# Layer 0's start: table rows in contiguous pieces, the second image's load on SyncE, tables between the first bands' pieces

## The chip, the cores and the metric

The kernel runs on one core of one Trainium2 chip. The metric is the device time of one execution in microseconds (us), given as the median of several runs. A core has five engines, each with its own instruction stream: TensorE (PE, matrix products and transposes), VectorE (DVE), ScalarE (ACT), GpSimd (POOL) and SyncE (SP, which here only issues DMAs). ScalarE can issue DMAs too; an instruction that issues one and has to wait holds up whatever stands behind it on its engine.

## What is computed

Two images x of 128 channels and 64 x 64 pixels go through two layers. Layer 0 is group norm, then a neighbourhood attention block (4 heads of 32 channels, each pixel looks at a 7 x 7 window, with a learned table of position biases rpb), then two small dense blocks. Layer 1 is a full attention over the 4096 tokens of each image and a spectral convolution in four branches.

```python
x = x + _L0_conv_ref(_gn(x), ...)              # layer 0
t = _to_tokens(x)
t = t + _L1_attn_ref(_ln_t(t))                 # layer 1
t = t + _L1_ffn_ref(_ln_t(t), ...)

# inside layer 0
y = _ln(x, g1, be1)
qkv = (y @ qkv_w.T + qkv_b)                    # q scaled by DH ** -0.5
attn = einsum('bnhwd,bnhwijd->bnhwij', q, Kw)  # Kw, Vw: 7 x 7 windows, moved inside at the border
attn = attn + rpb[:, bih, biw]                 # bih, biw: offset of key from query, 0 to 12
out = einsum('bnhwij,bnhwijd->bnhwd', softmax(attn), Vw)
y = out @ proj_w.T + proj_b
y = _ln(y, g2, be2) @ w1.T + bl1 + r           # r: layer 0's input, then two more dense products
```

The change touches only how the bias table is brought into place, when the second image is loaded, and in what order the first pieces of layer 0's work are issued.

## The kernel before, in words

Layer 0 works in bands of eight image rows, 512 pixels: eight bands for each of the two images, sixteen in all, numbered k = 0 to 15. A band is eight tiles of 8 x 8 pixels; two tiles make a unit, so a band has units u0 to u3. The keys of a tile are a window of 14 x 14 pixels (196). A band's work is cut into named pieces (functions under `@piece`). Those of the first part, called `p.`, are: xg (group norm applied), tok (transpose to tokens), bn, pw, nb, zd, za (layer norm on DVE, POOL, DVE, DVE and ACT), tr and zT (transpose back), then k, q, v (products) and kT, qT, vc (copies out of PSUM). Each unit then has S (scores), t0 to t3 (one per head: scores plus table, with the minimum, on DVE), e0 to e3 (exponential, on ACT), T0, T1 (transposes of p), c0, c1 (their copies) and V (product with v). `r.` and `t.` pieces finish a band; `k.` pieces begin layer 1 for the first image.

The order on PE, DVE, ACT and POOL is written out: every piece gets a time, all are sorted by it, and the engines follow that order. `PLAN` gives a piece's time in its band, and each band is shifted by PERIOD = 2300. The first pieces stand outside of it: the string `FIRST` lists them, and a name's place in it less 1000 is its time. In `FIRST`, `gn` is group norm of image 0, `w` and `wd` the small products that fold biases into weights, `f0` to `f3` bring the table of one head into place, `tab0` to `tab3` make the first table from it on DVE, and `tab` makes twelve more on POOL. Four further steps (`behind`, L747 on, driven by `rest_`) fold the remaining weights; they stand at the times 150, 500, 850 and 1200, that is among the pieces of unit 0 to unit 1 of band 0. `second` (at 1000) loads the second image into `xa[1]` in four pieces, issued by ScalarE (L795). SyncE's order is not written out: it takes its DMAs as they are issued and allowed.

The table. For each head, the host lays rpb into a padded array of RPR = 21 rows of RPW = 128 numbers. A query at row r, column q of its tile needs the 20 x 20 numbers that begin at its own offset in this array. They are loaded so that the query's place is the partition: `rev` has 64 partitions (eight rows r of eight q), and one partition holds, for each head, 20 rows of 20 numbers. For each r two DMAs do it: L290 (heads 1 to 3, on SyncE, or on ScalarE where r is 2 or 5) and L292 (head 0, on ScalarE), with runs of 20 numbers, 80 bytes. `rev` lies in the buffer `cm[0]`, which layer 1 uses later; what lies outside of the padded array is filled by the two memsets at L281 and L282. A product with the constant `flip` (L248) then reverses the order of the queries and doubles it to 128 partitions in PSUM, and ScalarE copies it to `base` (L252). `table` (L254 to L261) subtracts it from the window mask.

The keys and values. `p.vc` copies v and stores it in eight DMAs per band to DRAM (vd, L475), and `windows` (L485 on) loads for each unit four pieces of 7 rows x 14 columns x 128 channels back (vw, L492), sixteen for a band. There are six buffers of vw, four are used by a band. All of these DMAs are issued by SyncE. The rows of a window reach into the neighbouring bands, so a band's loads wait for the next band's stores.

Of the kernel before, what the change touches and what calls it, by code (L numbers as in the profile page):

```python
# [14 lines left out]
P = 128  # L15
# [5 lines left out]
HEADS, DH, KW = 4, 32, 7  # L21
# [9 lines left out]
W_QKV, W_PROJ, W_1, W_2, W_3 = 0, 384, 512, 640, 768  # L31
V_G1, V_BE1, V_G2, V_BE2, V_G3, V_BE3, V_G4, V_BE4, V_QB, V_KB, V_BL3 = range(11)
R_VB, R_PROJ, R_BL1, R_BL2 = range(4)
RPW = 128


QT, WN, NTAB = 8, 14, 20
# [2 lines left out]
BAND = QT * GW  # L40


RPR = NTAB + 1

# [23 lines left out]


FIRST = (
    "gn p.xg0 p.xg1 p.tok0 p.tok1 w p.bn0 p.bn1 p.pw0 p.pw1 p.zd0 p.nb0 p.za0 p.tr0 p.zd1 p.nb1 p.za1 wd p.xg2 p.zT0 f0"
    " p.tr1 f1 p.v0 p.q0 p.k0 p.zT1 p.vc0 p.qT0 tab0 p.kT0 f2 f3 tab p.v1 p.k1 p.q1 tab1 p.vc1 p.kT1 p.qT1 tab2 tab3"
).split()
PHW = P + TH

# [15 lines left out]
def kernel(  # L93
# [16 lines left out]
    nc = tc.nc  # L110
# [12 lines left out]
    xa = [xp.tile([P, T], F32, tag=f"xa{b}", name=f"xa{b}") for b in range(NB)]  # L123
    xin = x.rearrange("b c h w -> b c (h w)")
    for c in range(4):
# [3 lines left out]
    tt, tok, cm = [None, None], [None, None], [None, None]  # L129
# [4 lines left out]
    space = tok[0].rearrange("p n c -> p (n c)")  # L134
    base = space[:, 0 : HEADS * NTAB * NTAB].rearrange("p (h n m) -> p h n m", h=HEADS, n=NTAB)
    mask = space[:, HEADS * NTAB * NTAB : HEADS * NTAB * NTAB + 6 * KEYS].rearrange("p (c k) -> p c k", k=KEYS)
    rev = cm[0][0 : QT * QT, 0 : HEADS * RPR * NTAB].rearrange("p (h n m) -> p h n m", h=HEADS, n=RPR)

    ident = const.tile([P, P], F32, name="ident")
    make_identity(nc, ident)  # L140
# [4 lines left out]
        out=flip, in_=flip, compare_op=ALU.not_equal, fill=1.0, base=1 - QT * QT, pattern=[[0, 2], [1, QT * QT]],  # L145
# [73 lines left out]
    with l0a:  # L219
# [21 lines left out]
        tab = big.tile([P, 6, HEADS, KEYS], F32, name="tab")  # L241
        def l0_bank(kind=0):
            pool, tag = rings[kind]
            return pool.tile([P, 512], F32, tag=tag, name="bank")

        def flipped(h):
            pb = l0_bank()
            nc.tensor.matmul(  # L248
                pb[:, 0 : NTAB * NTAB], lhsT=flip.rearrange("p a q -> p (a q)"),
                rhs=rev[:, h, 0:NTAB].rearrange("p n m -> p (n m)"), start=True, stop=True,  # L250
            )
            nc.scalar.copy(base[:, h].rearrange("p n m -> p (n m)"), pb[:, 0 : NTAB * NTAB])  # L252

        def table(ci, h, eng):  # L254
# [16 lines left out]
            out=gavg, in_=gavg, compare_op=ALU.is_ge, fill=0.0, base=0,  # L271
# [3 lines left out]
            out=gavg, in_=gavg, compare_op=ALU.is_ge, fill=0.0, base=3,  # L275
# [2 lines left out]
        gavg = gavg.rearrange("p g r -> p (g r)")  # L278


        nc.gpsimd.memset(rev[:, 0].rearrange("p n m -> p (n m)"), 0.0)  # L281
        nc.gpsimd.memset(rev[:, HEADS - 1, NTAB], 0.0)  # L282
        nc.sync.dma_start(out=mask, in_=nc.inline_tensor(_window_masks(), "window_masks").ap())
        for r in range(QT):
            lo = 6 - min(r, 6)
            src = bass.AP(
                rpb_pad.tensor, (RPR + r - 6) * RPW + 50, [[1, QT], [RPW, (HEADS - 1) * RPR - r // 7], [1, NTAB]]
            )
            rows_ = rev[r * QT : (r + 1) * QT].rearrange("p h n m -> p (h n) m")
            (nc.scalar if r % 3 == 2 else nc.sync).dma_start(out=rows_[:, RPR : HEADS * RPR - r // 7], in_=src)  # L290
            src = bass.AP(rpb_pad.tensor, (lo + r - 6) * RPW + 50, [[1, QT], [RPW, RPR - lo], [1, NTAB]])
            nc.scalar.dma_start(out=rows_[:, lo:RPR], in_=src)  # L292
        wg = w_sb
        cb = wp.tile([P, 5], F32, name="cb")
        C_Q, C_K, C_V, C_1, C_3 = range(5)
# [476 lines left out]
        events = []  # L772
# [8 lines left out]
        for name, f in (  # L781
            ("gn", lambda: [None for _ in group_norm(0)]), ("w", weights), ("wd", weights_kept),
            *((f"f{h}", lambda h=h: flipped(h)) for h in range(HEADS)),
            *((f"tab{h}", lambda h=h: table(0, h, nc.vector)) for h in range(HEADS)),
            ("tab", lambda: [table(ci, h, nc.gpsimd) for ci in (1, 4, 5) for h in range(HEADS)]),
        ):
            events.append((FIRST.index(name) - 1000, None, "", f))
        for i in range(8):
            events.append((2 * PERIOD + 600 * i, None, "", lambda ci=2 + i // 4, h=i % 4: table(ci, h, nc.gpsimd)))
        rest_ = behind()  # L790
        for i in range(4):
            events.append((150 + 350 * i, None, "", lambda: next(rest_)))
        def second():
            for c in range(4):
                nc.scalar.dma_start(out=xa[1][:, c * 1024 : (c + 1) * 1024], in_=xin[1, :, c * 1024 : (c + 1) * 1024])  # L795

        events.append((1000, None, "", second))

        gn1 = group_norm(1)
        for i in range(7):  # L800
# [569 lines left out]
def _window_masks():  # L1370

    import numpy as np

    def seen(offset):

        q, k = np.arange(QT)[:, None], np.arange(WN)[None, :]
        lo = np.clip(offset + q - 3, 0, WN - KW)
        return (k >= lo) & (k < lo + KW)

    m = np.zeros((2, QT, QT, 6, WN, WN), np.float32)  # L1380
    for ci in range(6):
        rows_ = seen((0, 6, 3)[ci // 2])
        for ab in range(2):
            cols = seen(((0, 6), (3, 3))[ci % 2][ab])
            m[ab, :, :, ci] = np.where(rows_[:, None, :, None] & cols[None, :, None, :], 0.0, -MASKED)
    return m.reshape(P, 6, KEYS)
# [77 lines left out]
```

## Time and profile before

| what | value |
|---|---|
| median of 4 runs | 2264.2 us (2263.33 to 2265.31) |
| profiled execution | 2265.31 us |
| its span in the profile | 2263.6 us |
| granted PE clock, mean | 0.989 |
| DMA queue of SyncE | 177866 packets, 105.47 MB |
| DMA queue of ScalarE | 2840 packets, 2.27 MB |
| DMA issues L475 and L492 | 128 of 32.0 KB, 256 of 49.0 KB |

The profile gives, for each engine, how long it was busy, and for each idle stretch what ended it. A group of instructions is told by its line in the source, the engine, the operation and out<-in. Engine names with a q (SPq, ACTq) are the engines' issuing of DMAs. In a view of stretches, one row is a stretch of time, with the busy time of each engine in it, the clock that PE was granted as a share of full speed, and what the DMA engines moved. The chain of work goes back from the last instruction: at each step to what released it, or to the instruction before it on its engine. Layer 0 fills roughly the first 340 us of the span; the last band's window loads end at 328.

### The profile page before, as it was taken

Reading aid. Unit: us, or ns where it says so; the run is one execution under the profiler, and the core shown is the slowest. Engines: PE = TensorE matmul, PEld = TensorE weight load, DVE = VectorE, ACT = ScalarE, POOL = GpSimd, SP = SyncE. Lnnn points to the kernel's source line nnn. Section 1 sums busy time; section 2 is a strip of 40 time slices with the busy share of each in tenths; the row PEclk is TensorE's granted clock in tenths of the full one; section 3 lists DMA queues with packets and bytes.
Section 4 is the critical chain, followed back from the end, with each engine's and each line's share of the span. In section 5 each row is a group of like instructions: output and inputs, shape, how many; then the busy total and the mean of one; then the engine's idle time right before and its main releaser. Section 6 shows DMA issues by size and latency. Waiting matters only on the chain.

```text
span 2263.6 us, 31741 instructions
## 1 busy us (share of the span) xinstructions
PE 2186.1 (97%) x11908; PEld 1352.1 (60%) x11908; DVE 939.7 (42%) x3047; ACT 785.3 (35%) x1911; POOL 276.9 (12%) x354
## 2 busy tenths in 40 slices
PE   5899998999999999999999979999999999999998
PEld 3677764544544444544444436776677777767777
DVE  4799985432444346433333333222213222232323
ACT  2789883222333223222222323223223222232322
POOL 3367874200000000000000000000000000000000
PEclk8999999999999999999999989999999999999999
DMA  4222213011100015100000133122222121222101
GB/s 116 65 61 61 61 51 50 0 56 56 33 24 24 11 45 153 32 24 23 1 24 24 42 85 91 42 55 58 44 53 58 39 58 39 57 45 52 41 8 75
DMA packets 180858, 109.76 MB, mean 48 GB/s; under 512 B 32225, under 2 KB 165857, under 8 KB 180194
## 3 DMA queue, kind: packets, MB, share of 16 engines
q1 hardware_dynamic: 177866, 105.47, 18.0%
q10 hardware_dynamic: 2840, 2.27, 0.4%
q8 instruction: 94, 1.54, 0.3%
q14 instruction: 58, 0.48, 0.1%
HBM read 73.09 MB, written 34.60 MB: 48 GB/s over the span
## 4 chain that ended last, share of the span: by engine, by line
PE 87%; DVE 5%; POOL 3%; DMA 1%; ACT 1%; issue 1%; SPq 1%; POOLq 0%; DVEq 0%; ACTq 0%
PE acc L1288 25%; PE pc L1277 13%; PE bank L896 10%; PE own L924 10%; PE other L949 8%; PE bank L910 4%; PE bank L331 2%; PE py L1315 2%; PE bank L1041 2%; PE bank L188 2%; PE bank L1009 2%; PE bank L541 1%; PE bank L1150 1%; PE po L563 1%; PE bank L505 1%
## 5 line engine op out<-in xcount | busy, mean ns | idle before, releaser
L1278 DVE COPY y<-pc 128x512 f32<-128x512 f32 x320 | 221.4, 692 | 359.0 <-PE pc L1277 355.3
L903 ACT ACTIVATE e<-bank 128x512 f32<-128x512 f32 x288 | 171.8, 597 | 562.7 <-PE bank L896 426.8
L896 PE MATMUL bank<-cm 128*128 128x512 f32 x576 | 298.0, 601 | 1.4 <-DVE y L652 1.4
L1277 PE MATMUL pc<-ct,ut 64*128 64x512 f32 x1280 | 287.6, 599 | 5.9 <-issue 5.9
L1288 PE MATMUL acc<-y,mpl 128*128 128x256 f32 x1280 | 292.1, 382 | 0.0
L1288 PE MATMUL acc<-y,mmi 128*128 128x256 f32 x1280 | 288.0, 379 | 0.0
L1288 PEld LDWEIGHTS acc<-y,mpl 128*128 128x128 f32 x1280 | 238.1, 190 | 59.4 <-issue 29.6
L1288 PEld LDWEIGHTS acc<-y,mmi 128*128 128x128 f32 x1280 | 242.6, 190 | 32.7
L1278 ACT COPY y<-pc 128x512 f32<-128x512 f32 x320 | 205.2, 641 | 93.7 <-PE pc L1277 93.7
L949 PE MATMUL other<-e,tok 128*128 128x512 f32 x448 | 228.6, 592 | 0.0
L924 PE MATMUL own<-et,tok 128*128 128x512 f32 x448 | 226.9, 593 | 0.7 <-DVE part L913 0.7
L913 DVE CUSTOM_DVE_ANT_0 et<-bank,one 128x512 f32<-128x512 f32 x224 | 145.6, 688 | 164.9 <-PE bank L910 164.8
L1277 PEld LDWEIGHTS pc<-ct,ut 64*128 64x128 f32 x1280 | 122.0, 188 | 152.6 <-issue 147.4
L1294 ACT COPY ob<-acc 128x256 f32<-128x256 f32 x40 | 24.1, 603 | 430.9 <-PE acc L1288 430.9
L924 PEld LDWEIGHTS own<-et,tok 128*128 128x128 f32 x448 | 84.6, 190 | 108.3 <-issue 73.1
L949 PEld LDWEIGHTS other<-e,tok 128*128 128x128 f32 x448 | 85.0, 190 | 106.6 <-issue 105.9
L1327 DVE TENSOR_TENSOR xa<-py,xa 128x512 f32<-128x512 f32 x32 | 22.1, 692 | 281.4 <-PE py L1315 281.4
L896 PEld LDWEIGHTS bank<-cm 128*128 128x128 f32 x576 | 96.0, 193 | 71.2 <-issue 42.7
L910 PEld LDWEIGHTS bank<-ident,e 128*128 128x128 f32 x896 | 103.3, 141 | 54.0 <-issue 45.9
L160 POOL TENSOR_TENSOR ln_rs<-ln_rs,mhalf 128x4 f32<-128x4 f32 x24 | 24.3, 1011 | 869.4 <-DVE ln_rs L159 869.4
L528 ACT ACTIVATE p<-p,mn 128x196 f32<-128x196 f32 x256 | 114.4, 449 | 22.1 <-DVE mn L518 13.7
L910 PE MATMUL bank<-ident,e 128*128 128x128 f32 x896 | 116.9, 273 | 0.0
(200 smaller groups left out, 2338.1 us busy)
## 6 DMA issues: line engine op xcount, KB each, us to landing
ut<-us SPq DMA_DIRECT2D x80, 256.0 KB
us<-ub SPq DMA_DIRECT2D x64, 256.0 KB
vw<-vd SPq DMA_DIRECT2D x256, 49.0 KB
ct<-gs SPq DMA_DIRECT2D x160, 72.0 KB
ct<-gs SPq DMA_DIRECT2D x160, 64.0 KB
gs<-ub SPq DMA_DIRECT2D x20, 256.0 KB
vd<-v SPq DMA_DIRECT2D x128, 32.0 KB
st<-in_m_plus_dram SPq DMA_DIRECT2D x16, 256.0 KB
```

What stands on the lines that cost most here:

```text
L188: nc.tensor.transpose(ps[:, j * P : (j + 1) * P], src[:, j, :], ident)
L331: nc.tensor.matmul(pl, lhsT=wg[:, lo : lo + P], rhs=zT, start=True, stop=True)
L528: nc.scalar.activation(p, p, AF.Exp, bias=t[name + "mn"][:, h : h + 1], scale=-1.0, accum_out=t["den"][:, u, h : h + 1],)
L896: nc.tensor.matmul(ps, lhsT=cm[b][:, n * P : (n + 1) * P], rhs=cm[b][:, chunk(c)], start=True, stop=True)
L903: nc.scalar.activation(e, ps, AF.Exp, bias=0.0, scale=ASCALE, accum_out=part[:, n, c : c + 1])
L910: nc.tensor.transpose(pt[:, k * P : (k + 1) * P], es[k][:, m * P : (m + 1) * P], ident)
L913: nc.vector.tensor_tensor_reduce(et, pt, one, 1.0, 0.0, ALU.mult, ALU.add, part[:, n, a : a + 1])
L924: nc.tensor.matmul(own, lhsT=tok[b][:, n, :], rhs=e, start=first, stop=last)
L949: nc.tensor.matmul(other, lhsT=tok[b][:, 4 * CHUNKS[a] + j, :], rhs=es[j], start=(j == 0), stop=(j == 3))
L1277: nc.tensor.matmul(pc, lhsT=ut[fp, b, par, :], rhs=cv_[fp], start=True, stop=True)
L1278: (nc.scalar.copy if f else nc.vector.tensor_copy)(y[:, 4 * f : 4 * f + 4, :, par, b * 2 * FB + q : (b + 1) * 2 * FB : 2], pc.rearrange("p ...
L1288: nc.tensor.matmul(acc, lhsT=(mmi if l else mpl)[:, k, :], rhs=y[:, 1::2, k, ::-1, :] if l else y[:, 0::2, k, :, :], start=(l == 0 and k = ...
```

## The change

- RPW goes from 128 to 70 and RPR from 21 to 22, so that the padded rows lie closely and what a query needs of a head is one contiguous run of RLEN = 19 x 70 + 20 = 1350 numbers, 5400 bytes. `rev` becomes a list of four places: heads 1 and 2 in `cm[0]`, heads 0 and 3 in `tt[0]`, behind the 3 x 128 numbers that `behind` uses.
- For each r there is one DMA on SyncE (heads 1 and 2, two runs for each of eight partitions) and two on ScalarE (heads 0 and 3, one run for each of eight partitions; head 0's leaves out the rows before the array). One memset stays.
- The product of `f0` to `f3` reads its 20 x 20 numbers out of the run with a row step of 70.
- The second image's four loads go from ScalarE at the time 1000 to SyncE, right behind the row pieces and ahead of the first store of v; `second` is gone.
- In `FIRST`, f0 stands behind w, f1 behind p.za0, f2 behind p.zT0, f3 behind p.tr1, with tab after it; tab0, tab1 and tab2 stand ahead of p.kT0, tab3 ahead of p.v1.
- The four steps of `behind` go from 150, 500, 850, 1200 to 900, 1200, 1500, 1800.

```diff
-RPW = 128
+RPW = 70
-RPR = NTAB + 1
+RPR = NTAB + 2
+RLEN = (NTAB - 1) * RPW + NTAB
 FIRST = (
-    "gn p.xg0 p.xg1 p.tok0 p.tok1 w p.bn0 p.bn1 p.pw0 p.pw1 p.zd0 p.nb0 p.za0 p.tr0 p.zd1 p.nb1 p.za1 wd p.xg2 p.zT0 f0"
-    " p.tr1 f1 p.v0 p.q0 p.k0 p.zT1 p.vc0 p.qT0 tab0 p.kT0 f2 f3 tab p.v1 p.k1 p.q1 tab1 p.vc1 p.kT1 p.qT1 tab2 tab3"
+    "gn p.xg0 p.xg1 p.tok0 p.tok1 w f0 p.bn0 p.bn1 p.pw0 p.pw1 p.zd0 p.nb0 p.za0 f1 p.tr0 p.zd1 p.nb1 p.za1 wd p.xg2 p.zT0"
+    " f2 p.tr1 f3 tab p.zT1 p.v0 p.q0 p.k0 p.vc0 p.qT0 tab0 tab1 tab2 p.kT0 tab3 p.v1 p.k1 p.q1 p.vc1 p.kT1 p.qT1"
 ).split()
...
-    rev = cm[0][0 : QT * QT, 0 : HEADS * RPR * NTAB].rearrange("p (h n m) -> p h n m", h=HEADS, n=RPR)
+    place = tt[0].rearrange("p n c -> p (n c)")[0 : QT * QT, 3 * P :]
+    rev = [place[:, 0 : NTAB * RPW], *(cm[0][0 : QT * QT, h * RLEN : h * RLEN + NTAB * RPW] for h in range(2))]
+    rev.append(place[:, NTAB * RPW : 2 * NTAB * RPW])
...
-                rhs=rev[:, h, 0:NTAB].rearrange("p n m -> p (n m)"), start=True, stop=True,
+                rhs=rev[h].rearrange("p (n w) -> p n w", w=RPW)[:, :, 0:NTAB], start=True, stop=True,
...
-        nc.gpsimd.memset(rev[:, 0].rearrange("p n m -> p (n m)"), 0.0)
-        nc.gpsimd.memset(rev[:, HEADS - 1, NTAB], 0.0)
+        nc.gpsimd.memset(rev[0][:, 0 : 6 * RPW], 0.0)
         nc.sync.dma_start(out=mask, in_=nc.inline_tensor(_window_masks(), "window_masks").ap())
         for r in range(QT):
+            rows_ = slice(r * QT, (r + 1) * QT)
             lo = 6 - min(r, 6)
-            src = bass.AP(
-                rpb_pad.tensor, (RPR + r - 6) * RPW + 50, [[1, QT], [RPW, (HEADS - 1) * RPR - r // 7], [1, NTAB]]
-            )
-            rows_ = rev[r * QT : (r + 1) * QT].rearrange("p h n m -> p (h n) m")
-            (nc.scalar if r % 3 == 2 else nc.sync).dma_start(out=rows_[:, RPR : HEADS * RPR - r // 7], in_=src)
-            src = bass.AP(rpb_pad.tensor, (lo + r - 6) * RPW + 50, [[1, QT], [RPW, RPR - lo], [1, NTAB]])
-            nc.scalar.dma_start(out=rows_[:, lo:RPR], in_=src)
+            src = bass.AP(rpb_pad.tensor, (RPR + r - 6) * RPW + 50, [[1, QT], [RPR * RPW, 2], [1, RLEN]])
+            nc.sync.dma_start(out=cm[0][rows_, 0 : 2 * RLEN].rearrange("p (h e) -> p h e", e=RLEN), in_=src)
+            for h, n0 in ((0, lo), (HEADS - 1, 0)):
+                src = bass.AP(rpb_pad.tensor, (h * RPR + n0 + r - 6) * RPW + 50, [[1, QT], [1, RLEN - n0 * RPW]])
+                nc.scalar.dma_start(out=rev[h][rows_, n0 * RPW : RLEN], in_=src)
+        for c in range(4):
+            nc.sync.dma_start(out=xa[1][:, c * 1024 : (c + 1) * 1024], in_=xin[1, :, c * 1024 : (c + 1) * 1024])
...
-            events.append((150 + 350 * i, None, "", lambda: next(rest_)))
-        def second():
-            for c in range(4):
-                nc.scalar.dma_start(out=xa[1][:, c * 1024 : (c + 1) * 1024], in_=xin[1, :, c * 1024 : (c + 1) * 1024])
-
-        events.append((1000, None, "", second))
+            events.append((900 + 300 * i, None, "", lambda: next(rest_)))
```

## The prediction

> **What bounds the kernel now.** I read the page first. Over the whole span the matrix engine carries the chain of work, 87% of it, and it is busy 97%.
>
> ```profile
> PE 2186.1 (97%) x11908; PEld 1352.1 (60%) x11908; DVE 939.7 (42%) x3047; ACT 785.3 (35%) x1911; POOL 276.9 (12%) x354
> PE   5899998999999999999999979999999999999998
> PE 87%; DVE 5%; POOL 3%; DMA 1%; ACT 1%; issue 1%; SPq 1%; POOLq 0%; DVEq 0%; ACTq 0%
> ```
>
> The row of slices shows where there is anything to win: the first slice (57 us each) stands at 5 tenths, the second at 8. The change touches only these. So I cut the first 65 us into stretches (columns: stretch, length, busy us of PE, weight loads, DVE, ACT, POOL, granted PE clock, DMA share, GB/s).
>
> ```profile
> 10.00:15.00 5.00, 2.34 (x9) 2.00 (x10) 2.55 (x10) 0.00 (x0) 0.57 (x1) 1.00 0.83 84
> 15.00:20.00 5.00, 2.52 (x13) 2.42 (x11) 3.92 (x25) 1.33 (x2) 2.52 (x4) 1.00 0.75 41
> ...
> 45.00:50.00 5.00, 4.17 (x38) 2.41 (x26) 3.56 (x21) 0.94 (x3) 0.00 (x0) 0.50 0.60 176
> 50.00:55.00 5.00, 0.00 (x0) 0.00 (x0) 0.00 (x0) 0.60 (x3) 0.00 (x0) 0.50 0.53 161
> 55.00:60.00 5.00, 4.11 (x30) 2.58 (x34) 0.42 (x2) 4.47 (x17) 0.00 (x0) 0.50 0.68 230
> 60.00:65.00 5.00, 5.00 (x91) 3.60 (x81) 1.74 (x7) 2.05 (x4) 0.00 (x0) 0.87 0.08 23
> ```
>
> From 50 to 55 every compute engine stands still, and around it the PE clock is at half. The timeline says why.
>
> ```profile
> 46.39 0.45 ACT L405 ACTIVATE z<-bank,ln_nb,ln_rs 128x128 f32<-128x128 f32 x1
> 47.30 7.05 ACTq L795 DMA_DIRECT2D xa<-in_x_dram  x3
> 54.40 0.46 ACT L528 ACTIVATE p<-p,mn 128x196 f32<-128x196 f32 x1 [7.56 <-DMA vw<-vd]
> ```
>
> ScalarE issues the four loads of the second image (L795) in the middle of its work, and is idle 7.56 us. The releaser is a landing of vw. In the compiled program DMAs draw on eight semaphores in turn, and each waits for the landing of the last DMA that had its own; at that point these are window loads that SyncE is still issuing one by one. The e pieces of unit 1 (L528) stand behind, then everything else.
>
> SyncE is the second thing to watch.
>
> ```profile
> 28.67 10.53 SPq L475 DMA_DIRECT2D vd<-v  x16
> 39.24 22.87 SPq L492 DMA_DIRECT2D vw<-vd  x22
> 64.42 4.96 SPq L475 DMA_DIRECT2D vd<-v  x8
> ```
>
> A store costs it 0.61 us, a window load 0.79. Per band that is 8 x 0.62 + 16 x 0.79 = 17.6 us, and later bands begin their stores at 192.33, 210.12, 227.99: 17.8 apart, so SyncE is then all but full too.
>
> At the start the statistics of the image follow its four pieces; the first products run slowly, and before the first transposes PE sits idle.
>
> ```profile
> 4.68 2.54 DVE L339 BATCH_NORM_STATS2 gst<-xa 128x6 f32<-128x512 f32 x4 [3.61 <-DMA xa<-in_x_dram]
> 20.47 1.25 PE L188 MATMUL bank<-ident,z 128*128 128x128 f32 x4 [2.95 <-ACT z L405]
> 31.02 1.61 PE L248 MATMUL bank<-cm,flip 64*128 64x400 f32 x4
> ```
>
> The waits view charges ScalarE's first 18.66 us to cm; its last row load was issued at 16.2, and 18.66 follows the DVE's ln_nb (18.43 + 0.16) directly, so that one is what ended the wait.
>
> [...] eight L541 transposes take 1.95 us at 55.89 and 1.04 at 61.84, after the clock is back.
>
> **The change, part by part.** All shifts are against the profiled execution.
>
> 1. Row pieces. Before: eight pieces of 504 or 496 rows and eight short ones with 1176 together, so 5200 rows of 80 B, some 0.42 MB. After: 8 x 16 rows of 5400 B on SyncE (0.69 MB) and 16 pieces of 8 rows on ScalarE (0.64 MB): 256 rows, 1.33 MB. The image's pieces land 1.34 us apart (4.68, then 7.38 for the third), 524 KB each, so 391 GB/s, 24.4 KB/us per DMA engine. By the order of semaphores, four ScalarE pieces (19.9 KB per engine if on eight) need no wait and three more (13.7 KB) come before the image's last piece: 33.6 / 24.4 = 1.4 us on these engines, less what before's small rows took there. Bounds 0 and 1.4; I take +0.9, on the path, since the statistics follow the landing. The last pieces hang on a chain of landings (w, then the masks, then pieces in turn, each some 2 us); I get 16.5 us for head 0, 17.3 for head 3, 18.3 for heads 1 and 2. Eight engines carry 128 + 28 + 37 + 166 = 359 KB by then, 14.7 us from 2.5: 17.2, which agrees.
>
> 2. Tables early. f0 and f1 stand before tr0, f2 before tr1, f3 before v0. PE is free from 17.5, so at 18.4 with the delay. Four f at 1.63 us (21.65 to 23.28) and two transposes at 1.1 are 8.7: v0 at 27.2 instead of 25.95, +1.3. Two of the f are thereby moved from after k0, where they took 1.53 together: the third band's transposes come at 35.1 instead of 35.27. ScalarE loads its function table (1.28 us) ahead of f0's copy, when it waits anyway. SyncE's stores begin 1.3 later (30.0), sixteen take 9.8: first window load at 39.8, +0.6.
>
> 3. DVE. tab2 and tab3 (2.33 us at 35.40) no longer stand before the statistics of band 2 (37.77): they fit its idle time before 31. So t0 at 37.0 instead of 38.98, e0 at 37.4 instead of 39.36: -2.0. POOL's sixteen tables end near 36 instead of 41.06 and no longer hold band 2's root.
>
> 4. The `rest_` pieces, moved from 150 to 900 onward, no longer stand between e0 and unit 1. Before, the transposes of unit 0 waited for L759/L760 until 42.56 and unit 1's e could have begun at 46.95. After: e0 + 1.8 for four e, 1.9 for eight transposes, 0.6 copy, 0.85 z, 0.5 for scores: about 43. Their own work (some 2.6 us of DVE, 2 of PE) falls into units 1 and 2 and gives back some 1.5.
>
> 5. The second image's load. ScalarE's 7.56 us go. The four loads now wait on SyncE for row pieces, leave by about 18, and land by 24 (2.1 MB at 391 GB/s), before the first store at 30: nothing hides behind them. Group norm of image 1 starts far later (near 84).
>
> With 4 and 5, e of unit 1 begins near 43.2 instead of 54.40: -11.2; with the returned 1.5, unit 0's V at 49.8 instead of 59.47: -9.7.
>
> 6. What is late next: SyncE. 39.8 + 20 x 0.79 = 55.6, two more loads, 57.3: band 2's stores start then (v is there by 53: its copy followed the first e of unit 1 by 9.4, 54.40 to 63.81), not at 64.42: -7.1. Unit 0 of band 1 needs the fifth load behind these stores: 57.3 + 5.1 + 4.0 + 2.2 for landing (bounded by 124.71 + 4.0 to the use at 130.93) = 68.6 instead of 76.67: -8.1. PE would have been ready at 67.0, so SyncE decides. Afterwards it has a little slack (before averaged 18.3 per band against its 17.8), while PE and DVE are at 95 to 100%, so nothing more is won. Past this point the order of instructions is the same to the end, and the shift carries through.
>
> Sum: 2263.6 - 8.0 = 2255.6 for the span. The profiled run took 2265.31, the median of the four is 2264.2, so 0.6 over the span: **2256.2 us**.
>
> **Rivals.**
> - SyncE or the rows give back more of it. For: SyncE is back to back and starts its stores later. With +1.4 in step 1, PE at the slow clock and an extra wait for the rows of 1.5, stores slip 2.5 and the gain is 4.5 to 5: 2259.5.
> - More than that. For: PE no longer idles 6.55 us, [...] (half-clock PE work from 41 to 61 is some 12 us), and a first clock rise before 28 would bring the stores forward. Then -12: 2252.
> - The gain is lost further on: a later wait (image 1, the hand-over to layer 1) had its own end, in which layer 0 finishing early is slack. Against: there PE is 84 to 90% busy from 340 to 400 and its loads follow the same SyncE queue. No change: 2264.
> - Slower. The rows are not carried at the image's rate but at the rate of the stretch 15 to 20, 41 GB/s: 1.33 MB need 32 us, the last lands near 35. PE's order has f1 before tr0, so everything stands behind it: v0 some 15 late, minus the 8 to 10 won: +6, 2270. It decides from a landing of about 28 (53 GB/s). Against: rows of 80 B made that rate, these have 5400.
>
> **How the numbers follow.** The four-part case of -6 to -10.5: 0.58; -3 to -6: 0.14; beyond -10.5: 0.14; within 3: 0.08; slower: 0.06. What a measurement can tell from no change is 0.2%, 4.5 us. Faster takes the first, the third and half of the second: 0.79; same 0.15 with the other half; slower 0.06. The range from 2251 to 2261.5 leaves out the two last cases and the tails.
>
> **What would show it.** Right: no stretch without work between 45 and 55; the four image loads on SPq before 20; x's last statistics 1 us later; first f before the first L188; SyncE's third group of stores near 57 and no long gap before it. Wrong: f1 or f0 waiting on rows beyond 22; stores starting later than 32; PE waiting for vw by several us in band 1; a hand-over to layer 1 at the old time.

## The result and the profile after

The kernel after takes 2262.56 us (median of 36 runs), the one before, run beside it, 2264.85 (56 runs): a ratio of 0.9988, 95% interval 0.9983 to 0.9993. The change wins 2.3 us where 8 were forecast. The span of the profiled execution is 2261.0 us (before: 2263.6), at the same mean clock, 0.989.

Busy times, slices of PE and the shares of the chain, from the page of the kernel after. Nothing has moved outside of the first slices; the first is at 6 tenths instead of 5:

```profile
PE 2188.3 (97%) x11908; PEld 1354.2 (60%) x11908; DVE 939.8 (42%) x3047; ACT 785.1 (35%) x1911; POOL 276.8 (12%) x353
PE   6899998999999999999999979999999999999998
PE 88%; DVE 5%; POOL 3%; DMA 2%; ACT 1%; SPq 1%; issue 1%; POOLq 0%; DVEq 0%; ACTq 0%
```

The stretches of the kernel after (columns as before: PE, weight loads, DVE, ACT, POOL, clock, DMA share, GB/s):

```profile
10.00:15.00 5.00, 1.14 (x4) 1.00 (x4) 2.74 (x9) 0.00 (x0) 0.00 (x0) 1.00 0.71 214
15.00:20.00 5.00, 3.73 (x16) 3.42 (x16) 3.76 (x21) 0.68 (x1) 1.64 (x3) 1.00 0.46 109
...
45.00:50.00 5.00, 4.50 (x40) 3.06 (x39) 3.10 (x22) 3.24 (x13) 0.00 (x0) 0.50 0.19 55
50.00:55.00 5.00, 5.00 (x19) 3.98 (x19) 1.01 (x4) 2.13 (x9) 0.00 (x0) 0.50 0.22 65
55.00:60.00 5.00, 5.00 (x70) 3.11 (x68) 1.76 (x4) 2.25 (x5) 0.00 (x0) 0.92 0.22 64
60.00:65.00 5.00, 4.00 (x110) 2.73 (x95) 4.11 (x26) 4.39 (x18) 2.14 (x4) 1.00 0.26 69
```

The hole at 50 to 55 is filled. In ScalarE's timeline nothing stands any more between z (L409) and unit 1's e (L532), which begins at 47.70 instead of 54.40:

```profile
45.14 0.81 ACT L409 ACTIVATE z<-bank,ln_nb,ln_rs 128x128 f32<-128x128 f32 x2
47.70 0.46 ACT L532 ACTIVATE p<-p,mn 128x196 f32<-128x196 f32 x1 [1.76 <-DVE mn L522]
```

But SyncE's timeline shows that everything starts late. The first store of v is issued at 34.81 instead of 28.67 (forecast: 30.0), and band 2's stores at 62.10 instead of 64.42 (forecast: 57.3):

```profile
11.15 9.65 SPq L291 DMA_DIRECT2D cm<-in_rpb_pad_dram  x8
20.84 2.11 SPq L296 DMA_DIRECT2D xa<-in_x_dram  x4
34.81 9.93 SPq L479 DMA_DIRECT2D vd<-v  x16
44.78 17.22 SPq L496 DMA_DIRECT2D vw<-vd  x22
62.10 4.96 SPq L479 DMA_DIRECT2D vd<-v  x8
```

From its first store on SyncE makes no pause: 62.10 - 34.81 = 27.3 us. So the question is why the first store is 6.1 us late. DVE's timeline shows the first image's pieces landing 2.1 to 2.2 us apart, where they came 1.34 apart before:

```profile
4.72 1.28 DVE L343 BATCH_NORM_STATS2 gst<-xa 128x6 f32<-128x512 f32 x2 [3.66 <-DMA xa<-in_x_dram]
6.81 1.29 DVE L343 BATCH_NORM_STATS2 gst<-xa 128x6 f32<-128x512 f32 x2 [0.80 <-DMA xa<-in_x_dram]
9.03 1.29 DVE L343 BATCH_NORM_STATS2 gst<-xa 128x6 f32<-128x512 f32 x2 [0.93 <-DMA xa<-in_x_dram]
11.15 1.29 DVE L343 BATCH_NORM_STATS2 gst<-xa 128x6 f32<-128x512 f32 x2 [0.71 <-DMA xa<-in_x_dram]
```

And PE's timeline shows two more waits, ahead of f0 and of f1 (the products with flip; the brackets hold the idle time before one and its releaser):

```profile
12.99 0.56 PE L351 MATMUL bank<-gmv,gavg 128*128 128x1 f32 x2 [12.99 <-DVE gmv L346]
...
21.44 1.67 PE L252 MATMUL bank<-tt,flip 64*128 64x400 f32 x2 [1.46 <-DMA cm<-in_rpb_pad_dram]
25.14 1.67 PE L252 MATMUL bank<-cm,flip 64*128 64x400 f32 x2 [2.03 <-DMA xa<-in_x_dram]
...
32.08 2.07 PE L469 MATMUL bank<-w_sb,zT 128*128 128x128 f32 x8
```

The profile names xa as the releaser of f1, though f1 reads only head 1's rows in cm. In this trace the DMAs of SyncE and ScalarE count on eight semaphores (100 and 102 to 108), and one of those that f1 waits for, 100, counts a row piece (issued at 16.60) and then the first load of xa (issued at 20.84, counted from 24.64 on), so the name can be that of another transfer; I take it as a wait for the rows, whose last packet ended at 23.86 and whose landing was last counted at 25.01. The lines add up. The first group-norm product comes at 12.99 instead of 10.54: 2.45. The waits for rows are 1.46 + 2.03 = 3.49. Together 5.94 of the 6.13 by which v0 (L469) comes late, 32.08 instead of 25.95; 0.2 is left, at most, for the new order itself.

### The profile page after: what moved, and what is told of

Its sections match the earlier page's. It is cut to its first block, busy times and chain, and to the rows that moved or that the text cites. A ratio compares the mean times of both kernels' runs of the same rounds, so it can differ in the third digit from the quotient of the medians.

```text
span 2261.0 us, 31753 instructions
## 1 busy us (share of the span) xinstructions
PE 2188.3 (97%) x11908; PEld 1354.2 (60%) x11908; DVE 939.8 (42%) x3047; ACT 785.1 (35%) x1911; POOL 276.8 (12%) x353
## 3 DMA queue, kind: packets, MB, share of 16 engines
q1 hardware_dynamic: 175570, 108.02, 18.3%
## 4 chain that ended last, share of the span: by engine, by line
PE 88%; DVE 5%; POOL 3%; DMA 2%; ACT 1%; SPq 1%; issue 1%; POOLq 0%; DVEq 0%; ACTq 0%
PE acc L1287 25%; PE pc L1276 13%; PE bank L895 10%; PE own L923 10%; PE other L948 8%; PE bank L909 4%; PE py L1314 2%; PE bank L335 2%; PE bank L192 2%; PE bank L1040 2%; PE bank L1008 2%; PE bank L545 2%; PE bank L1149 1%; PE bank L509 1%; PE po L567 1%; DVE tt L977 1%
## 5 line engine op out<-in xcount | busy, mean ns | idle before, releaser
L532 ACT ACTIVATE p<-p,mn 128x196 f32<-128x196 f32 x256 | 114.4, 449 | 13.9 <-DVE mn L522 13.2
```

Source lines behind the costliest of these rows:

```text
L532: nc.scalar.activation(p, p, AF.Exp, bias=t[name + "mn"][:, h : h + 1], scale=-1.0, accum_out=t["den"][:, u, h : h + 1],)
```

## The experiments

All figures below are of the profiled run of each kernel, except the time: it is the median, as a difference from the kernel before in the same series. "Sums" is the start of the first group-norm product, "rows" the time that PE stood still for rows ahead of f products, "pause" SyncE's wait right ahead of band 2's stores. There is one profile for each kernel, and it can lie off the median, most in e8 (2262.29 against 2258.61).

| run | sums | rows | v0 | first store | band-2 stores | pause | time against before |
|---|---|---|---|---|---|---|---|
| before | 10.54 | 0 | 25.95 | 28.67 | 64.42 | 2.3 | 0 |
| after | 12.99 | 3.49 | 32.08 | 34.81 | 62.10 | 0 | -2.3 |
| e1_image_only | 10.56 | 0 | 25.98 | 28.70 | 56.08 | 0 | -7.4 |
| e3_old_rows | 11.25 | 1.86 | 28.38 | 31.10 | 58.35 | 0 | -4.0 |
| e5_image_late | 12.67 | 5.23 | 33.49 | 36.55 | 64.43 | 0 | +0.3 |
| e6_old_order | 12.87 | 0 | 28.28 | 31.00 | 61.64 | 2.1 | -2.8 |
| s1_four_loads | 10.78 | 0 | 26.19 | 28.91 | 58.10 | 0 | -5.8 |
| e8_half_by_act | 11.38 | 0 | 26.80 | 29.52 | 56.73 | 1.9 | -6.5 |
| r1_rows_aligned | 12.86 | 3.34 | 31.79 | 34.51 | 61.76 | 0 | -2.4 |
| r2_rows_overlap | 13.10 | 3.72 | 32.43 | 35.16 | 62.40 | 0 | -2.3 |
| w1_rows_spread | 12.64 | 3.54 | 31.84 | 34.56 | 61.82 | 0 | -3.5 |
| w6_spread_old_order | 12.74 | 0 | 28.14 | 30.86 | 60.08 | 2.1 | -3.6 |
| e7_rows_by_sync | 10.40 | 11.65 | 37.32 | 40.04 | 67.75 | 0 | +2.9 |
| e4_image_and_rest | 10.65 | 0 | 26.07 | 28.79 | 59.25 | 2.1 | -6.4 |
| w2_rows_merged | 10.37 | 6.27 | 31.90 | 34.62 | 61.80 | 0 | -2.8 |
| w3_merged_rest_early | 10.27 | 5.66 | 31.20 | 33.92 | 61.10 | 0 | -0.8 |
| w4_merged_f_split | 10.40 | 4.74 | 27.12 | 29.38 | 56.55 | 0 | -8.0 |
| w9_other_half | 10.74 | 3.43 | 29.25 | 31.98 | 59.16 | 0 | -3.3 |
| w10_other_half_split | 11.45 | 0 | 23.14 | 30.23 | 54.97 | 1.6 | -6.6 |
| w7_f_behind_v | 11.30 | 0 | 23.16 | 28.97 | 55.43 | 3.2 | -4.7 |

Two sums run through the table. v0 comes at 25.95 + (sums - 10.54) + rows, within 0.4, in all runs but w4, w10 and w7, in which no f product stands between the first transposes and v0. And where SyncE makes no pause and issues the same DMAs, band 2's stores come 27.2 to 27.9 after the first store.

How far can single profiles be trusted? Before, e1, e3, e4, s1, e8 and w7 have the same DMAs up to the sums, and their sums lie between 10.54 and 11.38, so less than 0.9 between two kernels shows nothing here. The seven kernels in which ScalarE issues long rows beside the image have 12.64 to 13.10, clear of all others (11.45 at most).

The time follows band 2's stores within 1.2 us in 14 of the 19 changed kernels. In e3, w3, w9, w10 and w7 it is 2 to 4.3 us longer. For w10 and w7 a reason is given below; for the other three it stays open.

### The load alone, and what the rest of the change takes back

The first series takes the parts of the change off one at a time. e1 is the kernel before with nothing but the load moved:

```diff
+        for c in range(4):                       # behind the old row pieces
+            nc.sync.dma_start(out=xa[1][:, c * 1024 : (c + 1) * 1024], ...)
...
-        events.append((1000, None, "", second))
```

> The kernel before with one part of the change: the second image's four loads go from ScalarE to SyncE, behind the old 80-byte row pieces. Theory A (the long row pieces are what costs; the moved image load is what gains): the start stays as before, stores of v begin near 28.7 us and window loads near 39.2, ScalarE's 7.56 us idle stretch is gone, band 2's stores begin near 57 instead of 64.42; 6 to 7.5 us faster than before (about 2257.5). Rival B (SyncE's queue takes over whatever the start does, so nothing is won beyond some 2.5 us): 2 to 3 us faster (about 2262). Rival C (the image's 2.1 MB behind the rows hold up the last row pieces): products of the table wait for rows past 25 us and the gain is 0 to 3 us.

Measured: 2257.49 us, ratio 0.9963 (0.9950 to 0.9977). SyncE's timeline of e1:

```profile
16.94 2.14 SPq L294 DMA_DIRECT2D xa<-in_x_dram  x4
28.70 10.06 SPq L477 DMA_DIRECT2D vd<-v  x16
38.80 17.18 SPq L494 DMA_DIRECT2D vw<-vd  x22
56.08 4.96 SPq L477 DMA_DIRECT2D vd<-v  x8
```

With before's first store and no stall, band 2's stores come 8.3 us early. The load alone is worth more than the whole change.

e3 is the kernel after with the old rows of 80 bytes; the image on SyncE, the new order and the later rest stay.

```diff
-RPW = 70
+RPW = 128      # with the old rev, row pieces and memsets
```

> The changed kernel with only the row pieces put back to runs of 80 bytes (image load on SyncE, new order of the tables, later rest steps all stay). Theory A: image 0's pieces land 1.3 us apart again, group norm's sums end near 10.0 instead of 12.5, v of band 0 is made near 27 instead of 32, stores begin near 30; 6 to 9 us faster than before (2256 to 2259). Rival B: about 2.5 us faster, as the changed kernel. Rival C: the first table product waits for rows until past 23 and the gain stays under 4 us.

2260.92, ratio 0.9979 (0.9972 to 0.9985). That misses the 2256 to 2259 of theory A. In the early places PE waits 1.86 us for the old rows too. With the sums 0.7 late, which is within what alike kernels differ by, that is v0's 2.4.

e5 is the kernel after with the image's load issued by ScalarE right behind f3's copy, so that it is not in flight with the rows.

```diff
-        for c in range(4):
-            nc.sync.dma_start(out=xa[1][:, c * 1024 : (c + 1) * 1024], ...)
...
+        events.append((FIRST.index("f3") - 999.5, None, "", second))   # second as in the kernel before
```

> The changed kernel with the second image's four loads issued by ScalarE right after the copy of the last head's table, so that nothing of it is in flight beside the row pieces. Theory A: image 0's pieces are as late as in the changed kernel (last sums at 12.5), the second table product still waits for its rows, until about 23 instead of 25.1; 3 to 5 us faster than before (2260 to 2262). Rival C: the rows land when they are needed (about 21), the second product waits for nothing, 5 to 7 us faster (2258 to 2260). Rival B: 2.5 us faster, as the changed kernel.

2265.14, ratio 0.9997 (0.9989 to 1.0005). None of the three forecasts holds. Rows are waited for 5.23 us though no second image is in flight, so it is not what makes them late. Why the wait is 1.7 us longer than in the kernel after is not shown.

e6 is the kernel after with the old FIRST.

> The changed kernel with the old order of the first pieces: the table products stand behind the transposes again, so rows that come late hold up fewer pieces. Long rows, image load on SyncE and later rest steps stay. Theory A in its two parts (late image pieces 2.5 us, rows awaited by products in front of the transposes some 3.5 us): only the second part shrinks, v of band 0 near 29 to 30 instead of 32, 4 to 5.5 us faster than before (about 2260). If only the late image pieces matter: no difference from the changed kernel. If only the order matters: 6 to 8 us faster.

2262.09, ratio 0.9987 (0.9980 to 0.9993). PE's timeline of e6: the first transposes, then f0, which waits for nothing any more (no bracket), and v0:

```profile
22.80 1.25 PE L192 MATMUL bank<-ident,z 128*128 128x128 f32 x4 [2.94 <-ACT z L409]
23.98 1.70 PE L252 MATMUL bank<-tt,flip 64*128 64x400 f32 x2
...
28.28 2.07 PE L469 MATMUL bank<-w_sb,zT 128*128 128x128 f32 x8
```

v0 is late by just what the sums are late, 2.33. So the long rows cost twice: by delaying the image (2.4), and by being waited for where the new order puts f0 and f1 ahead of the transposes (3.5, of which e3 has 1.9 with the old rows). In e6 a third loss shows: SyncE is through with its window loads at 59.5 and waits 2.1 us for band 2's v.

### Is SyncE's queue the end of the chain?

s1 adds four loads of 64 KB that nobody reads, behind the first eight stores of e1; e8 lets ScalarE issue every other store of bands 0 and 1.

```diff
+            if b == 0 and g == 0:                # s1, behind the stores of band 0
+                for c in range(4):
+                    nc.sync.dma_start(out=spare[:, c * 32 : (c + 1) * 32], in_=xin[1, :, ...])
...
-                nc.sync.dma_start(               # e8
+                (nc.scalar if b == 0 and g < 2 and i % 2 else nc.sync).dma_start(
```

> The kernel of e1_image_only with four more small loads (64 KB each, nobody reads them) issued by SyncE right behind the first eight stores of v. Theory A (from the first store on, SyncE issues without a pause and its queue sets when everything after it comes): each load takes a place in the queue of about 0.6 us, so the first window load, the third band's stores and the end come 2 to 2.5 us later than in e1: first window load at 41 (e1: 38.8), band-2 stores at 58.4 (56.1), time 2259.5 to 2260. Rival B (another engine's work sets it and SyncE has slack): band-2 stores within 0.5 of e1, time 2257 to 2258.

> The kernel of e1_image_only with every other one of the eight stores of v in bands 0 and 1 issued by ScalarE instead of SyncE. Theory A: SyncE is eight places shorter before the third band's stores, so up to 8 x 0.6 = 4.9 us are to be had; ScalarE pays 8 x some 0.7 us of issuing, which may delay its copies; band-2 stores at 52 to 54 (e1: 56.1), time 2253 to 2256. Rival B (SyncE has slack): first window load and band-2 stores move by less than 1 us, time 2257 to 2259, or later by what ScalarE's issuing costs.

s1: 2259.36, ratio 0.9975 (0.9964 to 0.9986). The four loads took 1.87 us of SyncE, and band 2's stores came at 58.10, 29.2 us after the first store instead of e1's 27.4. e8: 2258.61, ratio 0.9973 (0.9962 to 0.9983). SyncE's timeline of e8:

```profile
38.16 16.65 SPq L494 DMA_DIRECT2D vw<-vd  x20
56.73 4.96 SPq L477 DMA_DIRECT2D vd<-v  x8
```

It is through at 54.81 and waits 1.9 for band 2's v. So SyncE's queue sets band 2's stores in e1, but only by a little: at 56.7 band 2's own v is as late, and e8 gained nothing. For the kernel after, the same follows only from its SyncE making no pause. In time alone s1, e8 and e1 can't be told apart, as their intervals overlap.

### Why the long rows are slow

r1 and r2 read the rows from another place (the tables hold other values): r1 8 KB apart and aligned, r2 256 bytes apart, so overlapping. w1 writes a piece's eight rows to partitions r, r + 8, ... instead of 8r to 8r + 7; w6 is w1 with the old order.

```diff
-            src = bass.AP(rpb_pad.tensor, ..., [[1, QT], [RPR * RPW, 2], [1, RLEN]])
+            src = bass.AP(m_plus.tensor, ..., [[2048, QT], [16384, 2], [1, RLEN]])   # r1
+            src = bass.AP(m_plus.tensor, ..., [[64, QT], [2048, 2], [1, RLEN]])      # r2
...
-            rows_ = slice(r * QT, (r + 1) * QT)
+            rows_ = slice(r, QT * QT, QT)                                            # w1, w6
```

> The kernel after with the long rows read from another input: the same number and lengths of pieces, but each partition's row begins 8 KB after the one before and at a multiple of 4 KB, where in the kernel after the eight partitions' rows of a piece begin 4 bytes apart. The table's values are wrong by that. Theory D (the rows are slow because eight engines read overlapping, unaligned stretches of the same place): a row's packet falls from a median of 0.30 us to near 0.22, the last row pieces land by 18 to 19 instead of 25, f1 ends its wait by 20, first store of v at 32 instead of 34.8, time 2258 to 2260. Rival E (the length, the number of engines and the image's pieces beside them are the cost, wherever they are read): packets at 0.28 to 0.32, f1 near 25, time 2261.5 to 2263.

> As r1_rows_aligned, with the eight partitions' rows of a piece beginning 256 bytes apart (aligned, but overlapping as in the kernel after). The table's values are wrong by that. If the alignment is what makes rows slow, it is as r1 (packets near 0.22, time 2258 to 2260); if it is the overlap, as the kernel after (0.30, 2262).

> The kernel after with the eight rows of a piece written to partitions r, r+8, ..., r+56 instead of 8r to 8r+7 (and the reversing matrix to match); sizes, numbers and queues of the pieces are the same. Theory G (rows are slow because the eight rows of a piece go into eight neighbouring partitions, [...] and they hold up the image's packets there): a row's packet falls from 0.27 to 0.30 us to near 0.22, the group-norm sums come at 11 to 11.5 instead of 13.0, f1 by 19 instead of 25, v0 at 27 to 29 instead of 32, first store at 30 to 32, band-2 stores at 57.5 to 59.5, time 2256 to 2259. Rival H (it is the piece with eight packets for eight engines, wherever they land): packets 0.27 to 0.30, sums near 13, time 2261 to 2263.

> The same spread with the old order of layer 0's start (the kernel of e6_old_order with rows spread). Theory G: sums at 11 to 11.5 (e6: 12.9), v0 at 26.5 (28.3), first store at 29.2 (31.0), band-2 stores at 58 to 60 (61.6), time 2257.5 to 2260. Rival H: as e6, 2262.

None of the four did what theories D and G ask for; against the kernel of the same order the sums moved by 0.35 us at most: 2262.75 (0.9985 to 0.9998), 2262.82 (0.9982 to 0.9995), 2262.28 (0.9976 to 0.9990), 2262.22 (0.9977 to 0.9990). By the packets in the traces, the median one of 5400 bytes took 0.35 us in the kernel after, 0.36 in r1, 0.35 in r2 and 0.34 in w1, and none fell to near 0.22. Neither where a row is read nor which of the 64 partitions it is written to is the main cause.

e7 has all the row pieces issued by SyncE, behind the first image.

```diff
-                nc.scalar.dma_start(out=rev[h][rows_, n0 * RPW : RLEN], in_=src)
+                nc.sync.dma_start(out=rev[h][rows_, n0 * RPW : RLEN], in_=src)
```

> The kernel after with the sixteen row pieces of ScalarE issued by SyncE too, so that all rows stand behind the first image on one queue. Theory F (the image's pieces come late because row pieces of another queue run beside them): statistics again 1.3 us apart, group-norm sums at 10.5 to 11. The rows then start later, and f1 comes at 22 to 26; v0 at 29 to 33, time 2258 to 2263. If the image's pieces come late for another reason, sums near 13 as in the kernel after.

2268.67, ratio 1.0012 (1.0006 to 1.0019): slower than before. DVE's timeline of e7 has six of the eight statistics without a gap, and the sums come at 10.40:

```profile
4.55 3.97 DVE L343 BATCH_NORM_STATS2 gst<-xa 128x6 f32<-128x512 f32 x6 [3.49 <-DMA xa<-in_x_dram]
```

That is theory F: ScalarE's row pieces, in flight beside the image, are what held it up. The price is larger than forecast (f1 at 22 to 26, 2258 to 2263 us): PE now stands 11.65 us ahead of f0, which comes at 29.04, as the rows have not come. Short stretches of the kernel after, beside the image and with rows alone:

```profile
6.00:8.00 2.00, 0.00 (x0) 0.00 (x0) 1.20 (x3) 0.00 (x0) 0.00 (x0) 1.00 1.01 249
...
14.00:16.00 2.00, 0.58 (x2) 0.50 (x2) 0.60 (x4) 0.00 (x0) 0.57 (x1) 1.00 0.48 91
16.00:18.00 2.00, 1.75 (x8) 1.54 (x9) 1.65 (x7) 0.00 (x0) 0.00 (x0) 1.00 0.47 117
```

and of e7, image alone and rows alone:

```profile
6.00:8.00 2.00, 0.00 (x0) 0.00 (x0) 1.86 (x4) 0.00 (x0) 0.00 (x0) 1.00 0.99 387
...
18.00:20.00 2.00, 0.00 (x0) 0.00 (x0) 1.47 (x9) 0.00 (x0) 0.93 (x1) 1.00 0.51 82
```

The last two columns say it. Beside rows the engines are just as full and move 249 GB/s instead of 387 (the stretches around it, 330 and 344 instead of 403 and 404). With rows alone the share is a half, and 82 to 117 GB/s are moved. That half of the engines is at work all the time, and not all of them half of the time, shows in the packets: in e7, from 12.2 to 24, exactly eight were under way in 93% of all moments (in the kernel after, from 20 to 22, in 81%), where the image has about sixteen (in the kernel after 16.1 in the mean from 4 to 6). So each of the eight carries 10 to 15 KB/us, where the image has 24.

w2 brings the same rows in 11 transfers instead of 24: one for each of heads 1, 2 and 3, one for head 0 from its row 6 on, seven small ones, all behind the image on SyncE.

```diff
+        for h in (1, 2):                         # and the same for head 3
+            src = bass.AP(rpb_pad.tensor, at + (h - 1) * RPR * RPW, [[RPW, QT], [1, QT], [1, RLEN]])
+            nc.sync.dma_start(out=rev[h][:, 0:RLEN], in_=src)
```

> The kernel after with the same rows in few large pieces: one transfer of all 64 partitions for each of heads 1, 2, 3 and for head 0 from row 6 on (64 packets each), and seven small ones of eight partitions for head 0's rest, all on SyncE behind the first image; the second image behind them. Bytes and row lengths as before, 11 transfers instead of 24. Theory K (a piece of eight partitions has packets for eight engines only and moves some 11 KB/us on each; pieces of 64 partitions use all sixteen at the image's 24 KB/us): 1.3 MB at some 390 GB/s is 3.5 us, so the rows land by 14 to 15 instead of 25, the sums of the group norm come at 10.5 to 11, f0 and f1 wait for nothing, v0 comes at 26 to 27.5, the first store at 28.7 to 30.2, band-2 stores at 56 to 59.5, time 2257 to 2260. Rival L (rows of 5400 B are slow in any piece): rows land at 22 or later, f1 near 25, time 2261 or more.

2261.84, ratio 0.9989 (0.9981 to 0.9997). Of theory K only a part holds. Stretches of w2:

```profile
14.00:16.00 2.00, 2.00 (x11) 1.98 (x11) 1.65 (x10) 0.00 (x0) 0.00 (x0) 1.00 0.53 122
16.00:18.00 2.00, 1.35 (x6) 1.25 (x6) 1.57 (x12) 0.00 (x0) 1.62 (x4) 1.00 0.48 116
```

w2's large transfers are half as fast again as e7's small ones (122 against 82 GB/s), but still half of the engines stand idle (share 0.53), and f0 comes at 23.62 (e7: 29.04). w9 puts heads 0 and 3 into the other 64 partitions, and loads the heads in the order 1, 3, 2, 0:

```diff
-    place = tt[0].rearrange("p n c -> p (n c)")[0 : QT * QT, 3 * P :]
+    place = tt[0].rearrange("p n c -> p (n c)")[QT * QT : P, 3 * P :]   # flip likewise in both halves
```

> The kernel of w2_rows_merged with the rows of heads 0 and 3 in partitions 64 to 127 instead of 0 to 63 (and the reversing matrix in both halves). Theory M (which DMA engines carry a row follows from the partition it is written to, so 64 partitions leave half of the engines idle): the share of the engines between 12 and 16 us rises from 0.51 to near 1, the rows land by 16 to 17 instead of 20 to 21, f0 comes at 17 to 19 (w2: 23.6), v0 at 28 to 30 (33), first store at 30 to 32 (34.6), band-2 stores at 57.5 to 59.5, time 2257 to 2259.5. If the number of rows in a transfer sets it: share 0.51, rows as in w2, time as w2, 2261 to 2263.

2261.51, ratio 0.9984 (0.9978 to 0.9991); a stretch of w9:

```profile
14.00:16.00 2.00, 2.00 (x9) 1.79 (x10) 1.65 (x7) 0.00 (x0) 0.00 (x0) 1.00 0.50 159
```

Share 0.50: theory M falls as well, though each engine now moves more than in w2 (159 against 122 GB/s in all). Whether that comes from the place or from the order of the heads is not shown. What is left among the causes I thought of is the shape of the transfer. In w2 and w9 the outer dimension of the source is still 8 (r), as in every long piece of the kernel after, and all of them show a share near 0.5 (from 14 to 18: 0.47 to 0.53), where the image and the masks, with 128 partitions, have 1.01 to 1.07 (before, 4 to 10). The 80-byte pieces of the kernel before have an outer dimension of 8 too, yet the share was 0.82 to 0.92 from 12 to 18, and SyncE's queue alone had up to 16 of their packets under way at once. A long row in a transfer with an outer dimension of 16 was not tried. So that eight engines carry the long rows is shown; why it is eight, and why each carries 10 to 20 KB/us and not 24, stays open.

### The moved rest and the order, with rows out of the way

e4 is e1 with the later due times of the rest; w3 is w2 with the old ones. The rest are the four steps of `behind`, which fold weights; e4's forecast describes them wrongly as tokens and keys of later bands.

```diff
-            events.append((150 + 350 * i, None, "", lambda: next(rest_)))
+            events.append((900 + 300 * i, None, "", lambda: next(rest_)))    # e4; w3 the reverse
```

> The kernel of e1_image_only with the change's later due times for the four bands' tokens and keys behind the first (the moved rest). Theory A (they stand beside the path): 2256.5 to 2258.5, band-2 stores at 56 as in e1. Rival R (with the old order they come too late, and band 2's values are waited for, as e6 showed 2.1 us before its third group of stores): band-2 stores at 57.5 to 59, time 2259 to 2260.

> The kernel of w2_rows_merged with the moved rest back at its old due times, since e4_image_and_rest lost 1.9 us by it: band-2 stores at 55.5 to 57 without a wait for v, time 2256 to 2258. If the rest's place does not matter beside fast rows, as w2_rows_merged.

e4: 2259.40, ratio 0.9967 (0.9955 to 0.9979), an interval that overlaps e1's. Its trace shows rival R: SyncE stops at 57.15 and waits 2.1 us for band 2's v. The three kernels with the old order and a late rest (e4, e6, w6) all have this wait, those with the new order do not. w3: 2263.77 (0.9988 to 1.0001) where 2256 to 2258 was forecast, though its trace has band 2's stores 0.7 earlier than w2's. Its time does not fit the chain, and what makes it slower further on stays open.

w4 is w3 with f0 and f1 early and all else in the old order; w10 is w9's rows with f1 and f3 early, f0 behind the first k, f2 where tab wants it and the rest at its old times; w7 is e1 with f0 and f1 behind the first q and k.

```diff
-... p.xg2 p.zT0 f0 p.tr1 f1 p.v0 p.q0 p.k0 p.zT1 p.vc0 p.qT0 tab0 ...
+... w f0 ... p.za0 f1 p.tr0 ... p.zT0 p.tr1 p.v0 p.q0 p.k0 p.zT1 p.vc0 p.qT0 tab0 ...   # w4
+... w f1 ... p.za0 f3 p.tr0 ... p.zT0 p.tr1 p.v0 p.q0 p.k0 f0 p.zT1 p.vc0 p.qT0 ...     # w10
+... p.zT0 p.tr1 p.v0 p.q0 p.k0 f0 p.zT1 p.vc0 f1 p.qT0 tab0 ...                         # w7
```

> The kernel of w3_merged_rest_early with only f0 and f1 in their new early places and everything else of layer 0's start in the old order, so that two products fewer than in the kernel before stand between the sums and v0. If the rows are there by 15 (theory K), these two products fill TensorE's pause before tr0 and v0 comes 1.5 to 2 us earlier than before's 25.95, at 24 to 24.5; first store at 26.7 to 27.2, time 2254 to 2256.5 if SyncE's chain holds, 2257 if band 2's values, which are computed just ahead of their stores, become the bound. With theory L, 2260 or more.

> The kernel of w9_other_half in the order of w4_merged_f_split, with the products of heads 1 and 3, whose rows land first, in the two early places, those of heads 0 and 2 behind the first k, and the rest at its old due times. With theory M the two early products lie in TensorE's pause before tr0: v0 at 24 to 25, first store at 26.7 to 27.7, band-2 stores at 54 to 56, time 2254 to 2256.5. If the rows are as in w2: v0 at 26 to 27, 2256 to 2257.5.

> The kernel of e1_image_only with the old 80-byte rows and only f0 and f1 moved: from before v0 to behind the first q and k. Nothing of the first stores then waits for rows or products. Theory A (v0 and the first store set the end, at first store + 27.3 for band 2's): v0 at 23.5 to 24.5 instead of 25.98, first store at 26.3 to 27.2, band-2 stores at 53.7 to 55.5, time 2254.5 to 2256.5. If the tables, now later, or band 2's own values take over: band-2 stores at 56 and 2257 to 2258.5.

w4: 2256.61, ratio 0.9964 (0.9952 to 0.9977), though PE still waits 4.74 us for head 0's rows, for which 2260 or more was forecast. w10: 2258.24 (0.9963 to 0.9982). w7: 2260.16 (0.9973 to 0.9986). Both are later than either of their forecasts. In w10 and w7 v0 comes 2.8 us before that of the kernel before, but the first store does not follow: I had put f0's copy ahead of v's copy on ScalarE, and f0 comes after q and k. SyncE's timeline of w7 shows the second obstacle:

```profile
28.97 9.93 SPq L477 DMA_DIRECT2D vd<-v  x16
38.95 13.27 SPq L494 DMA_DIRECT2D vw<-vd  x17
55.43 4.96 SPq L477 DMA_DIRECT2D vd<-v  x8
60.50 17.01 SPq L494 DMA_DIRECT2D vw<-vd  x21
77.61 4.96 SPq L477 DMA_DIRECT2D vd<-v  x8
```

SyncE is through at 52.22 and waits 3.2 us for band 2's v. But only 17 window loads stand ahead of these stores, in w10 too, where the other kernels have 22; the five that are left are issued behind them. So an early band 2 says little here: band 3's stores come at 77.61 in w7 and 77.71 in w10, against 74.30 in e1, and with that goes the later end (w7's 2260.16 against e1's 2257.49). As band 2's v is not ready before 55 to 57 in w10, w7 and e8, an earlier v0 would need an earlier band 2 as well. w4 and e1 have the lowest times of all; their intervals overlap, and e1 is one move of four lines.

## Why the prediction was wrong

The step that failed is step 1. It took the image's pieces 0.9 us late (bounds 0 and 1.4) and the last rows landing at 16.5 (head 0), 17.3 (head 3) and 18.3 (heads 1 and 2). Both rest on 24.4 KB/us for each DMA engine, the image's rate. Measured: the sums 2.45 late, f0 released at 21.4 and f1 at 25.1. e7 shows that ScalarE's pieces beside the image are the cause of the first, e6 that waiting in the early places is the second, and the stretches that an engine carries rows at 10 to 15 KB/us. The eight engines, an assumption then, were right (e7's packets); the rate was borrowed from another shape. The packets show the same for the first: of the seven row pieces that step 1 put ahead of the image's last packet only five were there, 25.3 KB on each of eight engines instead of 33.6, and yet that packet ended at 10.41 instead of 8.27. That is some 12 KB/us; the delay broke the upper bound of 1.4 with fewer bytes than it was made for. And the 24 row pieces took 2.0 to 6.6 us each from issue to landing, 4.5 in the median, where step 1's chain of landings had some 2. Two of the prediction's own signs of being wrong came true: f1 waited beyond 22 (25.14) and the stores started later than 32 (34.81).

- Step 2's own size was about right. It had the order cost 0.4 of its 1.3, and at most 0.2 is left for it in the trace. Its v0 of 27.2 lacked 1.55 from the sums and 3.49 from rows: 32.2, against 32.08. Its start of the stores was wrong by this alone.
- Steps 3 and 4 were right in direction. Unit 0's e came at 41.09 and unit 1's at 47.70, later than the 37.4 and 43.2 forecast, by 3.7 and 4.5 us, a little less than v0's 4.9. That the later rest is free holds only with the new order.
- Step 5 was right and was the whole gain: ScalarE's stall is gone, and e1 gives 7.4 us for it. The loads left at 20.84 instead of 18, still well ahead of the first store.
- Step 6 was right as a mechanism: SyncE without a pause, 57.3 - 30.0 = 27.3 us after its first store, measured 27.3. Its first store was 4.8 late, and so were band 2's stores. The parts agree too (stores 9.9 us, forecast 9.8; window loads 17.2, forecast 17.5), so it is not two errors that cancel.

In time: 4.8 of the 6.4 between 2256.2 and 2262.6 come through band 2's stores, 0.6 more lies in the span, and 1.0 in what lies between span and median (1.6 instead of 0.6): the profiled run before was 1.1 us above its median, the one after 0.1.

Among the rivals the first had the true mechanism, a later image and an extra wait for rows, with a slip of the stores of 2.5 instead of 4.8. The last had the true danger, rows slower than the image, but with 41 GB/s where the kernel after has 91 to 135, and from a landing (28) that was not reached. What I should have done is let the landing of rows carry the uncertainty: f1 is in front of the transposes in PE's order, so each us of landing after some 20 is a us of v0, and no line of the trace before had a rate for such a piece.

The prediction's two lengths of the same transposes (1.95 and 1.04) show that the products took about twice as long at half clock, not what makes the clock fall. In the trace before it fell at 40.84, after PE had stood still for 2.89 us (to 40.21) and had had only one-column products just ahead of that, and was back at 61.32. In the trace after it fell at 42.19, after 1.59 us without work (to 41.69), and was back at 55.84, though PE was busy all of the time from 50 to 55. How much of this the idle time makes is not shown, and the rival of -12 was an estimate. No sum of the forecast rests on it.

## What to carry to other kernels

A transfer that moves off a busy engine is worth what its wait cost there, and can be tried alone: here it gave 7.4 us for a stall of 7.56, three times the gain of the change it came in. Putting a product that needs a load ahead of the work that is ready turns the load's landing into the path (3.49 us of waiting in the kernel after); put it behind, as long as its result is not needed. A rate from one shape of transfer was not a rate for another (24 KB/us for each engine with the image, 10 to 15 with the row pieces): the share of the DMA engines and the GB/s of a stretch (0.51 and 82 in e7), read together, hint at how many engines are at work and how fast; counting the packets under way (eight, in 93% of e7's moments) settles it.

## What was not expected of the hardware

- Fewer, longer runs were not quicker. 5200 rows of 80 bytes (0.42 MB) kept the DMA engines at a share of 0.8 to 0.9 and were in place in time; 256 rows of 3.7 to 5.4 KB (1.33 MB, with the gaps between the wanted numbers) kept half of them busy until 24.
- The same long rows went at 73 to 88 GB/s in 24 small transfers on one queue (e7), 91 to 135 on two queues (after), 116 to 130 in 11 transfers (w2) and 154 to 159 with two heads in the other partitions (w9), always at a share near 0.5 (0.41 to 0.55).
- Row packets of ScalarE's queue beside the image on SyncE's slowed it while all engines stayed full: from 6 to 8 the engines moved 249 GB/s at a share of 1.01 (after), instead of 387 at 0.99 (e7).
